# Softmax, normalising and gelu: small columns in one ring of buffers for each kind of column, where there was one ring for each width

## The chip, the cores and the metric

The kernel runs on one core of a Trainium2 chip. The metric is the device time in microseconds. It is one program, launched once. TensorE (PE) multiplies matrices into PSUM; VectorE (DVE), ScalarE (ACT) and GpSimd (POOL) do the rest, each from a queue of its own; SyncE (SP) issues transfers, and POOL issues the ones that gather or scatter rows.

## The reference

A gated block with cross-attention and a quantised feed-forward part, for 16 batches of 224 tokens with 512 numbers each, and a context of 750 rows of 384 numbers, of which a mask drops some:

```python
def _layernorm(x, axis=-1, eps=1e-05):
    m = jnp.mean(x, axis=axis, keepdims=True)
    v = jnp.var(x, axis=axis, keepdims=True)
    return (x - m) / jnp.sqrt(v + eps)

# _L0_xattn_ref: 8 heads of 64
q = (x @ W_q); k = (context @ W_k); v = (context @ W_v)
sim = jnp.where(mask, q k^T * scale, -max); attn = softmax(sim)
out = (attn @ v) @ W_o + b_o

# _L0_ffn_ref: both layers are bitlinear, with exact gelu between
def bitlinear(x, w, b):
    xq = act_quant(rmsnorm(x))     # scale 127 / max|x| of the row, rounded
    wq = weight_quant(w)           # -1, 0, 1 by the mean of |w|
    return jnp.einsum('bsd,fd->bsf', xq, wq) + b

x = x + jnp.tanh(g_xattn[0]) * _L0_xattn_ref(_layernorm(x), ctx_768, mask, ...)
x = x + jnp.tanh(g_ffn[0]) * _L0_ffn_ref(_layernorm(x), w1, b1, w2, b2)
return x
```

(The attention lines are shortened here.) What matters for the change is how many numbers there are of which each row has just one: a mean, a variance, a reciprocal of a softmax sum, a largest absolute value, a scale. Each is a column of 128 rows and one to six numbers.

## The kernel before

Batches are sorted by how many context rows their mask keeps. The eight fullest work with 192 key positions, the others with 128 (`CAPS`). If no batch has more, `compact_path` runs; it is the path that was profiled. It is one long list of instructions without loops on the chip.

The work is a pipeline of 16 stages, one for each batch `s`. A stage merges three streams of pieces by the costs written beside each piece (`merge`):

- `attention_pieces(s)`: softmax of the last two units of the batch and its weighted sum. A batch has four units `(s, n)`; a unit is 112 queries by four heads. `scores` (L1037) multiplies queries by keys, adds the mask with a running minimum on DVE (L1061), takes the exponential on ACT with its sum (L1071, `sum`), the reciprocal on DVE (L1080, `rec`) and multiplies by it on POOL (L1081). `turn_probs` transposes the result on TensorE (L1101, L1108).
- the `other` stream, which prepares later batches: `norm` (L944) for x of batch s+2, `gather` and `select` for its context rows, keys, values and queries for batch s+1. x comes in pairs of two 128-token tiles, by a gathering transfer that POOL issues (`fetch`, L793), into three buffers. `norm` takes statistics on DVE (`bs_x`, L952, then `mv_x`, L953), the scale and the negated mean on POOL (`rs_x`, `ls_x`, L956 to L959), and normalises x in place on POOL (L961).
- the `flow` stream. In stage 0 it rounds and transposes the weights w1, in stage 1 w2 (`weight_pieces`); `scale_weights` (L1371) adds the partial sums of |w| (`wtot`, L1373), spreads the total by a matmul with ones (L1375) and makes the scale; `round_weights` (L1392) and `turn_weights` (L1401) follow in eight pieces. From stage 2 on, it carries one pair of token tiles a stage through the feed-forward part: `residual`, `project` (L1184, output projection of the attention), `normalise` (L1213: `bs_y`, `mv_y`, `fx`, `a1`, `k`, the transposing transfer L1237, `r`, `c`), `up` (L1250), `gelu` (L1272: L1279 gelu on ACT, L1282 largest value `a2`, quantising, the transposing transfer L1288, L1290 squares on ACT with their sum `ss`, then `r2` and `c2` on POOL), `down` (L1300) and the scatter of the rows to the output (L1310).

After the last stage, the two last pairs are finished alone: `project` and `normalise` of pair 13, `up` and `gelu` of pairs 12 and 13, then `down`.

The order of the work on each engine is not written out in the kernel. The compiler takes the instructions in the order of the code as their priority, and moves a later one ahead when its inputs are ready and its engine has nothing to do by the compiler's own reckoning. A tile takes a buffer of its tag (its ring) when its first instruction is placed, and this can be only when a tile before it in that buffer has been read for the last time. [...]

All small columns come from one helper, which makes a tag of the width:

```python
    def small(name, n=2):
        return pa.tile([P, n], F32, tag=f"s{n}", name=name, bufs=24 if n == 2 else 6)
```

So there are three rings. The ring of two columns has 24 buffers and holds `rs`, `ls`, `k`, `c`, `a1`, `a2`, `r1`, `r2`, `ss`, `wtot`, `wmean`. The ring of four columns has six buffers and holds `mv` of x and of y, `sum` and `rec`. The ring of six columns has six buffers and holds `bs` of x and of y. PSUM has two wide buffers for scores, weighted sums and `up`, and four others (`gen`) for all else.

Of the kernel before, what the change touches and what calls it, by code (L numbers as in the profile page):

```python
# [8 lines left out]
F32 = mybir.dt.float32  # L9
# [716 lines left out]
def compact_path(ctx, tc, sh, x, context, out, late_loads):  # L726

    nc = tc.nc
    P = 128
    B, S, D = x.shape  # L730
    _, J, C = context.shape
# [17 lines left out]
    pa = ctx.enter_context(tc.tile_pool(name="pa", bufs=1))  # L749
# [21 lines left out]
    def wide(shape, dtype, name):  # L771
        return ps_sim.tile(shape, dtype, tag="sim", name=name)
# [6 lines left out]
    def pow_half(dst):  # L779
        nc.gpsimd.tensor_tensor(dst, dst, sh.mhalf[:, : dst.shape[1]], ALU.pow)  # L780

    def small(name, n=2):
        return pa.tile([P, n], F32, tag=f"s{n}", name=name, bufs=24 if n == 2 else 6)


    def token(t):
# [157 lines left out]
    def norm(i, ks=(0, 1)):  # L944

        xp = normed[i]
        name = f"x{i}_{ks[0]}"
        part = slice(ks[0], ks[-1] + 1)
        mv = small(f"mv_{name}", 4).rearrange("p (k n) -> p k n", k=2)
        for k in ks:  # L950
            st = small(f"bs_{name}_{k}", 6)
            nc.vector.bn_stats(st, xp[:, k, :])  # L952
            nc.vector.bn_aggr(mv[:, k, :], st)  # L953
            load["v"] += 850
        rstd = small(f"rs_{name}")
        nc.gpsimd.tensor_scalar(rstd[:, part], mv[:, part, 1], 1.0, EPS, ALU.mult, ALU.add)  # L956
        pow_half(rstd[:, part])
        less = small(f"ls_{name}")
        nc.gpsimd.tensor_scalar(less[:, part], mv[:, part, 0], -1.0, 0.0, ALU.mult, ALU.add)  # L959
        for k in ks:  # L960
            nc.gpsimd.tensor_scalar(  # L961
                xp[:, k, :], xp[:, k, :], less[:, k : k + 1], rstd[:, k : k + 1], ALU.add, ALU.mult
            )

    def norm_first(k):

        xp = normed[0]
        st = small(f"bs_x0_{k}", 6)
        nc.vector.bn_stats(st, xp[:, k, :])
        mv = small(f"mv_x0_{k}", 4)  # L970
        nc.vector.bn_aggr(mv[:, :2], st)
        rstd = small(f"rs_x0_{k}")
        nc.vector.tensor_scalar(rstd[:, :1], mv[:, 1:2], EPS, None, ALU.add)
        power = nc.gpsimd.tensor_tensor(rstd[:, :1], rstd[:, :1], sh.mhalf[:, :1], ALU.pow)
        nc.vector.tensor_scalar(xp[:, k, :], xp[:, k, :], mv[:, 0:1], rstd[:, :1], ALU.subtract, ALU.mult)
        return power.ins
# [60 lines left out]
    def scores(s, n):  # L1037
        st = live[s]
        cap = CAPS[s]
        q, u = UNITS[n]  # L1040
        sim = wide([TQ, 2, 2, 256], F32, f"sim_{s}_{n}")

        begin = P if cap > P else 0
        for i in range(2):
            p = 2 * u + i
            for j in range(2):
                nc.tensor.matmul(  # L1047
                    sim[:, j, i, :cap],
                    lhsT=st["qT"][j * DH : (j + 1) * DH, p, q * TQ : (q + 1) * TQ],
                    rhs=st["kT"][j * DH : (j + 1) * DH, p, j * begin : j * begin + cap],  # L1050
                    start=True,
                    stop=True,
                )
        probs = pa.tile([TQ, 4, 192], F32, tag="p", name=f"p_{s}_{n}", bufs=3)
        total = small(f"sum_{s}_{n}", 4)
        for i in range(2):
            for j in range(2):
                h = 2 * i + j
                nmax = pa.tile([TQ, 1], F32, tag="nm", name=f"nm_{s}_{n}_{h}", bufs=12)

                nc.vector.tensor_tensor_reduce(  # L1061
                    out=probs[:, h, :cap],
                    in0=sim[:, j, i, :cap],
                    in1=st["mask"][:, j * begin : j * begin + cap],
                    scale=-(DH**-0.5),
                    scalar=FMAX,
                    op0=ALU.add,
                    op1=ALU.min,
                    accum_out=nmax,
                )  # L1070
                nc.scalar.activation(  # L1071
                    probs[:, h, :cap],
                    probs[:, h, :cap],
                    AF.Exp,
                    bias=nmax,
                    scale=-1.0,
                    accum_out=total[:TQ, h : h + 1],
                )
        rec = small(f"rec_{s}_{n}", 4)
        nc.vector.reciprocal(rec[:TQ], total[:TQ])  # L1080
        nc.gpsimd.tensor_tensor(  # L1081
            probs[:, :, :cap],
            probs[:, :, :cap],
            rec[:TQ].unsqueeze(2).to_broadcast([TQ, 4, cap]),
            ALU.mult,
        )
        load["v"] += 4 * (150 + 1.05 * cap + 83) + 150
        load["s"] += 4 * (250 + 0.96 * cap + 187)
        st["p", n] = probs
# [106 lines left out]


    def quantiser(amax, part, least, name):
        k = small(f"k_{name}")
        nc.vector.tensor_scalar(k[:, part], amax[:, part], least, 1.0 / 127.0, ALU.max, ALU.mult)  # L1200
        nc.vector.reciprocal(k[:, part], k[:, part])
        load["v"] += 300
        return k

    def unquantiser(amax, r, part, isw, name):

        c = small(f"c_{name}")
        nc.gpsimd.tensor_tensor(c[:, part], amax[:, part], r[:, part], ALU.mult)
        nc.gpsimd.tensor_scalar(c[:, part], c[:, part], 1e-5, None, ALU.max)
        nc.gpsimd.tensor_scalar(c[:, part], c[:, part], isw, None, ALU.mult)  # L1210
        return c

    def normalise(i, ks=(0, 1)):  # L1213
        f = pairs[i]
        y = f["y"]
        name = f"{i}_{ks[0]}"
        part = slice(ks[0], ks[-1] + 1)
        mv = small(f"mv_y{name}", 4).rearrange("p (k n) -> p k n", k=2)
        if ks[0] == 0:
            f["fx"] = late["rows"].tile([P, 2, D], F32, tag="hq", name=f"fx_{i}", bufs=3)  # L1220
            f["xq"] = pa.tile([P, 2, D], BF16, tag="xq", name=f"xq_{i}", bufs=3)
            f["xqT"] = pa.tile([P, 2 * ND, P], BF16, tag="xq", name=f"xqT_{i}", bufs=3)
        fx, xq, xqT = f["fx"], f["xq"], f["xqT"]
        for k in ks:
            st = small(f"bs_y{name}_{k}", 6)
            nc.vector.bn_stats(st, y[:, k, :])
            nc.vector.bn_aggr(mv[:, k, :], st)
            nc.vector.tensor_scalar(fx[:, k, :], y[:, k, :], mv[:, k, 0:1], None, ALU.subtract)  # L1228
        amax = small(f"a1_{name}")
        nc.vector.tensor_reduce(amax[:, part], fx[:, part, :], AX.X, ALU.max, apply_absolute_value=True)  # L1230

        scale = quantiser(amax, part, 1e-5 * EPS, f"1_{name}")

        for k in ks:
            nc.vector.tensor_scalar(xq.bitcast(I16)[:, k, :], fx[:, k, :], scale[:, k : k + 1], None, ALU.mult)
        nc.vector.tensor_copy(xq[:, part, :], xq.bitcast(I16)[:, part, :])
        nc.sync.dma_start_transpose(  # L1237
            out=xqT[:, ks[0] * ND : (ks[-1] + 1) * ND, :], in_=xq[:, part, :].rearrange("p n d -> p (n d)")
        )

        r = small(f"r1_{name}")
        nc.gpsimd.tensor_scalar(r[:, part], mv[:, part, 1], 1.0 + EPS, EPS * EPS, ALU.mult, ALU.add)
        pow_half(r[:, part])
        c = unquantiser(amax, r, part, sh.isw[0], f"1_{name}")
        for k in ks:
            f["c1", k] = c[:, k : k + 1]
            nc.gpsimd.tensor_tensor(y[:, k, :], y[:, k, :], sh.b2, ALU.add)  # L1247
        load["v"] += len(ks) * (850 + 340 + 667 + 450 + 220)
# [23 lines left out]
    def gelu(i, ks=(0, 1)):  # L1272
        f = pairs[i]
        name = f"{i}_{ks[0]}"
        part = slice(ks[0], ks[-1] + 1)
        ss = small(f"ss_{name}")
        amax = small(f"a2_{name}")
        for k in ks:
            nc.scalar.activation(f["h", k], f["h", k], AF.Gelu)  # L1279
        for k in ks:  # L1280
# [7 lines left out]
            nc.sync.dma_start_transpose(out=hqT, in_=hq)  # L1288
        for k in ks:
            nc.scalar.activation(f["h", k], f["h", k], AF.Square, accum_out=ss[:, k : k + 1])  # L1290
        r = small(f"r2_{name}")
        nc.gpsimd.tensor_scalar(r[:, part], ss[:, part], 1.0 / FF, EPS, ALU.mult, ALU.add)
        pow_half(r[:, part])
        c = unquantiser(amax, r, part, sh.isw[1], f"2_{name}")
# [74 lines left out]
    weight_scale = [None, None]  # L1369

    def scale_weights(wi):  # L1371
        tot = small(f"wtot_{wi}")
        nc.vector.tensor_reduce(tot[:, 0:1], weight_sums[wi], AX.X, ALU.add)  # L1373
        pt = gen([P, 1], F32, f"wtotp_{wi}")
        nc.tensor.matmul(pt, lhsT=sh.ones, rhs=tot[:, 0:1], start=True, stop=True)  # L1375
        mean = small(f"wmean_{wi}")
        nc.vector.tensor_scalar(mean[:, 0:1], pt, 1.0 / (FF * D), 1e-5, ALU.mult, ALU.max)
        sw = pa.tile([P, 1], F32, name=f"sw_{wi}")
        nc.vector.reciprocal(sw, mean[:, 0:1])
# [205 lines left out]
```

## Time and profile before

| | |
|---|---|
| three timed runs | 758.72, 762.57, 763.36 us, median 762.57 |
| the profiled execution | 755.32 us, its span 753.5 us |
| mean granted TensorE clock | 0.976 |
| busy, share of the span | PE 90%, DVE 67%, ACT 54%, POOL 53% |
| instructions | PE 3902, DVE 1300, ACT 960, POOL 543 |
| read and written in HBM | 32.26 MB and 7.34 MB, 53 GB/s over the span |

The page divides the span in 40 slices of 18.8 us and gives each engine's busy share in tenths, with the clock that TensorE was granted (PEclk). The windows give the same as microseconds. In the timeline a line is start, duration, engine, line of the kernel and operation, with the tiles written and read; a number in square brackets is the time that the engine stood idle just before, and what ended it. Names of tiles there have lost their numbers, so `mv_x` stands for every pair of x. One and the same line of a helper can carry many operations: L766 and L763 are copies out of PSUM on ACT and DVE, L780 is the power of minus one half on POOL.

### The profile page before, as it was taken

Reading aid. Unit: us, or ns where it says so; the run is one execution under the profiler, and the core shown is the slowest. Engines: PE = TensorE matmul, PEld = TensorE weight load, DVE = VectorE, ACT = ScalarE, POOL = GpSimd, SP = SyncE. Lnnn points to the kernel's source line nnn. Section 1 sums busy time; section 2 is a strip of 40 time slices with the busy share of each in tenths; the row PEclk is TensorE's granted clock in tenths of the full one; section 3 lists DMA queues with packets and bytes.
Section 4 is the critical chain, followed back from the end, with each engine's and each line's share of the span. In section 5 each row is a group of like instructions: output and inputs, shape, how many; then the busy total and the mean of one; then the engine's idle time right before and its main releaser. Section 6 shows DMA issues by size and latency. Waiting matters only on the chain.

```text
span 753.5 us, 11378 instructions
## 1 busy us (share of the span) xinstructions
PE 680.1 (90%) x3902; PEld 432.9 (57%) x3902; DVE 505.9 (67%) x1300; ACT 407.6 (54%) x960; POOL 397.0 (53%) x543
## 2 busy tenths in 40 slices
PE   4997799999999999997999999999999999988652
PEld 3875587666566566555655575666666666443221
DVE  5598765877484784665768676588594939586860
ACT  1556564384663855736657369266565656460530
POOL 6583567464564644647266564565654453536141
PEclk9998999999999999999999999999999999999887
DMA  6874031132223322222142323123122222213150
GB/s 193 314 267 156 11 90 45 15 73 56 69 47 70 82 56 57 67 57 81 28 99 67 71 67 68 32 77 80 58 57 70 56 70 57 71 28 77 35 113 31
DMA packets 87218, 58.77 MB, mean 78 GB/s; under 512 B 75488, under 2 KB 75632, under 8 KB 87024
## 3 DMA queue, kind: packets, MB, share of 16 engines
q1 hardware_dynamic: 79024, 32.00, 18.8%
q0 software_dynamic: 8128, 25.96, 11.1%
q8 instruction: 33, 0.54, 0.3%
q14 instruction: 33, 0.27, 0.1%
HBM read 32.26 MB, written 7.34 MB: 53 GB/s over the span
## 4 chain that ended last, share of the span: by engine, by line
PE 57%; DVE 12%; issue 10%; POOL 9%; DMA 5%; ACT 2%; POOLq 0%; ACTq 0%; DVEq 0%; SPq 0%
PE qp L1008 9%; PE op L1189 9%; PE fp L1304 8%; PE hp L1259 6%; PE kp L892 5%; PE sim L1047 4%; PE vp L907 4%; PE ptp L1101 3%; PE av L1126 3%; DVE a L1282 2%; POOL p L1081 2%; DVE h L1267 2%; DMA raw<-in_L_ffn_w_dram 2%; DMA hqT<-hq 2%; DVE hq L1285 1%
## 5 line engine op out<-in xcount | busy, mean ns | idle before, releaser
L1081 POOL TENSOR_TENSOR p<-p,rec 112x768 f32<-112x768 f32 (+1 forms) x64 | 84.2, 1318 | 74.8 <-DVE rec L1080 29.6
L1304 PE MATMUL fp<-w2T,hqT 128*128 128x512 fp8e4 x448 | 104.2, 387 | 13.8 <-DMA hqT<-hq 13.7
L1259 PE MATMUL hp<-w1T,xqT 128*128 128x512 fp8e4 x448 | 107.0, 383 | 8.8 <-DVE h L1267 6.2
L1071 ACT ACTIVATE p<-p,nm 112x192 f32<-112x192 f32 (+1 forms) x256 | 106.4, 419 | 11.5 <-DVE nm L1061 11.3
L1008 PE MATMUL qp<-xnT,wq_sb 128*128 128x224 f32 x512 | 104.9, 358 | 0.6 <-ACT xnT L766 0.6
L1189 PE MATMUL op<-wo_sb,xoT 128*128 128x512 f32 x224 | 103.7, 599 | 0.0
L1008 PEld LDWEIGHTS qp<-xnT,wq_sb 128*128 128x128 f32 x512 | 96.8, 193 | 6.4 <-issue 3.3
L1267 DVE SCALAR_TENSOR_TENSOR h<-hp,c,b_bc 128x1024 f32<-128x1024 f32 x56 | 71.6, 1280 | 39.9 <-PE hp L1259 37.4
L1061 DVE CUSTOM_DVE_ANT_0 p<-sim,mask 112x192 f32<-112x192 f32 (+1 forms) x256 | 67.7, 319 | 33.9 <-PE sim L1047 33.4
L1304 PEld LDWEIGHTS <-hqT 128*128 128x128 bf16 x448 | 43.3, 99 | 71.0 <-DMA hqT<-hq 16.9
L1282 DVE TENSOR_REDUCE a<-h 128x1 f32<-128x2048 f32 x28 | 63.9, 2282 | 22.4 <-ACT h L1279 22.3
L1259 PEld LDWEIGHTS <-xqT 128*128 128x128 bf16 x448 | 43.2, 98 | 57.7 <-issue 15.4
L1308 DVE SCALAR_TENSOR_TENSOR y<-fp,c,y 128x512 f32<-128x512 f32 x28 | 20.9, 746 | 76.3 <-PE fp L1304 73.0
L1310 POOL DMA_INDIRECT out_dram<-y,token x28 | 30.9, 1104 | 75.6 <-DVE y L1308 70.6
L1290 ACT ACTIVATE h<-h 128x2048 f32<-128x2048 f32 x28 | 53.4, 1907 | 22.1 <-DVE hq L1285 14.7
L1279 ACT ACTIVATE h<-h 128x2048 f32<-128x2048 f32 x28 | 53.5, 1909 | 19.6 <-DVE k L1200 10.6
L1189 PEld LDWEIGHTS op<-wo_sb,xoT 128*128 128x128 f32 x224 | 40.6, 190 | 38.9 <-issue 36.4
L892 PE MATMUL kp<-ctxT,wk_sb 128*128 128x192 f32 (+1 forms) x384 | 60.9, 306 | 0.0
L892 PEld LDWEIGHTS kp<-ctxT,wk_sb 128*128 128x128 f32 x384 | 55.2, 192 | 6.2 <-issue 4.3
L1247 POOL TENSOR_TENSOR y<-y,b_bc 128x512 f32<-128x512 f32 x28 | 36.6, 1311 | 37.9 <-DVE fx L1228 37.6
L766 ACT COPY pT<-ptp 128x448 f32<-128x448 f32 x63 | 32.7, 536 | 42.6 <-PE ptp L1101 41.3
L1101 PE MATMUL ptp<-ident,p 112*128 112x112 f32 x256 | 36.1, 268 | 17.6 <-POOL p L1081 17.5
(165 smaller groups left out, 1191.4 us busy)
## 6 DMA issues: line engine op xcount, KB each, us to landing
raw<-in_L_ffn_w_dram SPq DMA_DIRECT2D x16, 512.0 KB, 5.6
wq_sb<-in_L_xattn_W_q_dram SPq DMA_DIRECT2D x1, 1024.0 KB, 5.8
b_bc<-in_L_ffn_b_dram SPq DMA_DIRECT2D x1, 1024.0 KB, 7.8
wk_sb<-in_L_xattn_W_k_dram SPq DMA_DIRECT2D x1, 768.0 KB, 7.4
wv_sb<-in_L_xattn_W_v_dram SPq DMA_DIRECT2D x1, 768.0 KB, 8.8
wo_sb<-in_L_xattn_W_o_dram SPq DMA_DIRECT2D x1, 512.0 KB, 3.8
wo_sb<-in_L_xattn_W_o_dram SPq DMA_DIRECT2D x2, 256.0 KB, 5.6
x<-in_x_dram,token POOLq DMA_INDIRECT x28, 3.6
```

The costliest lines, as they stand in the source:

```text
L892: nc.tensor.matmul(pk[:, p - p0, :], lhsT=sh.wk[:, c, p * P : (p + 1) * P], rhs=st["ctxT"][:, c, :cap], start=(c == 0), stop=(c == NC - 1),)
L1008: nc.tensor.matmul(pq[:, i, :], lhsT=sh.wq[:, d, (p + i) * P : (p + i + 1) * P], rhs=st["xnT"][:, d, :], start=(d == 0), stop=(d == ND - 1),)
L1061: nc.vector.tensor_tensor_reduce(out=probs[:, h, :cap], in0=sim[:, j, i, :cap], in1=st["mask"][:, j * begin : j * begin + cap], scale=-(DH ...
L1071: nc.scalar.activation(probs[:, h, :cap], probs[:, h, :cap], AF.Exp, bias=nmax, scale=-1.0, accum_out=total[:TQ, h : h + 1],)
L1081: nc.gpsimd.tensor_tensor(probs[:, :, :cap], probs[:, :, :cap], rec[:TQ].unsqueeze(2).to_broadcast([TQ, 4, cap]), ALU.mult,)
L1101: nc.tensor.transpose(pt[:, h, :], probs[:, h, c : c + P], ident[:TQ, :TQ])
L1189: nc.tensor.matmul(po, lhsT=xoT[:, d, at : at + P], rhs=sh.wo[:, d, :], start=(d == 0), stop=(d == ND - 1))
L1259: nc.tensor.matmul(ph[:, n, :], lhsT=f["xqT"][:, k * ND + d, :], rhs=w1T[:, d, at : at + NB], start=(d == 0), stop=(d == ND - 1),)
L1267: nc.vector.scalar_tensor_tensor(h[:, cols], ph.rearrange("t i n -> t (i n)"), f["c1", k], sh.b1[:, cols], ALU.mult, ALU.add)
L1279: nc.scalar.activation(f["h", k], f["h", k], AF.Gelu)
L1282: nc.vector.tensor_reduce(amax[:, k : k + 1], h, AX.X, ALU.max, apply_absolute_value=True)
L1304: nc.tensor.matmul(po, lhsT=f["hqT", k][:, n, :], rhs=w2T[:, n, :], start=(n == 0), stop=(n == NF - 1))
```

## The change

The helper takes a kind and a name. The kind is the tag, so each kind has a ring of its own, and every ring has six buffers, whatever its width. The rest of the change gives a kind to each call: `mvx`, `bsx`, `rsx`, `lsx` for x; `sum` and `rec` for softmax; `mvy`, `bsy`, `a1`, `k1`, `r1`, `c1` for the normalising; `ss`, `a2`, `k2`, `r2`, `c2` for gelu; `wtot` and `wmean` for the weights. These are 19 rings and 114 buffers, where there were three rings and 36 buffers. No operation, engine, operand or transfer is another.

```diff
-    def small(name, n=2):
-        return pa.tile([P, n], F32, tag=f"s{n}", name=name, bufs=24 if n == 2 else 6)
+    def small(kind, name, n=2):
+        return pa.tile([P, n], F32, tag=kind, name=f"{kind}_{name}", bufs=6)
...
-        mv = small(f"mv_{name}", 4).rearrange("p (k n) -> p k n", k=2)
+        mv = small("mvx", name, 4).rearrange("p (k n) -> p k n", k=2)
         for k in ks:
-            st = small(f"bs_{name}_{k}", 6)
+            st = small("bsx", f"{name}_{k}", 6)
...
-        rstd = small(f"rs_{name}")
+        rstd = small("rsx", name)
...
-        less = small(f"ls_{name}")
+        less = small("lsx", name)
...
-        total = small(f"sum_{s}_{n}", 4)
+        total = small("sum", f"{s}_{n}", 4)
...
-        rec = small(f"rec_{s}_{n}", 4)
+        rec = small("rec", f"{s}_{n}", 4)
...
-        k = small(f"k_{name}")
+        k = small("k" + name[0], name[2:])
...
-        c = small(f"c_{name}")
+        c = small("c" + name[0], name[2:])
...
-        mv = small(f"mv_y{name}", 4).rearrange("p (k n) -> p k n", k=2)
+        mv = small("mvy", name, 4).rearrange("p (k n) -> p k n", k=2)
...
-            st = small(f"bs_y{name}_{k}", 6)
+            st = small("bsy", f"{name}_{k}", 6)
...
-        amax = small(f"a1_{name}")
+        amax = small("a1", name)
...
-        r = small(f"r1_{name}")
+        r = small("r1", name)
...
-        ss = small(f"ss_{name}")
-        amax = small(f"a2_{name}")
+        ss = small("ss", name)
+        amax = small("a2", name)
...
-        r = small(f"r2_{name}")
+        r = small("r2", name)
...
-        tot = small(f"wtot_{wi}")
+        tot = small("wtot", wi)
...
-        mean = small(f"wmean_{wi}")
+        mean = small("wmean", wi)
```

The three columns of `norm_first`, which normalises the first pair of x at the very start, take the same kinds as those of `norm`.

More of the change, by code (lines that the diff above doesn't have):

```diff
@@ L967, in norm_first @@
         xp = normed[0]
-        st = small(f"bs_x0_{k}", 6)
+        st = small("bsx", f"x0_{k}", 6)
         nc.vector.bn_stats(st, xp[:, k, :])
-        mv = small(f"mv_x0_{k}", 4)
+        mv = small("mvx", f"x0_{k}", 4)
         nc.vector.bn_aggr(mv[:, :2], st)
-        rstd = small(f"rs_x0_{k}")
+        rstd = small("rsx", f"x0_{k}")
         nc.vector.tensor_scalar(rstd[:, :1], mv[:, 1:2], EPS, None, ALU.add)
```

## The prediction

> **What bounds the kernel now.** I read the page's busy times first, then its slices, then the windows of the early slices, and only then the order of single instructions in the timeline. All of it is one profiled execution of 755.32 us (span 753.5 us, the rest lies around it). The three timed runs have a median of 762.57, so I work out a difference and apply it to both.
>
> ```profile
> PE 680.1 (90%) x3902; PEld 432.9 (57%) x3902; DVE 505.9 (67%) x1300; ACT 407.6 (54%) x960; POOL 397.0 (53%) x543
> PE   4997799999999999997999999999999999988652
> PEclk9998999999999999999999999999999999999887
> ```
>
> TensorE is the bound nearly everywhere: 9 or more in 31 of 40 slices. It falls short at the start, in slices 4 and 5, in slice 19 and in the last six. A change of little columns on DVE, ACT and POOL can gain only where TensorE waits for them, so those slices are all there is to win. In the windows (columns: stretch, sum of the stretch, PE, PEld, DVE, ACT, POOL busy with counts, granted clock, DMA) the early shortfall is 5.1 us and 4.7 us, and the clock is short there as well:
>
> ```profile
> 56.50:75.30 18.80, 13.72 (x78) 9.58 (x77) 15.74 (x31) 12.19 (x29) 6.82 (x6) 0.82 0.49 156
> 75.30:94.20 18.90, 14.20 (x129) 10.86 (x128) 14.24 (x49) 11.22 (x33) 9.93 (x10) 0.91 0.04 11
> 113.00:131.90 18.90, 18.80 (x137) 14.28 (x135) 10.74 (x47) 9.23 (x30) 14.80 (x16) 1.00 0.16 45
> ```
>
> The stretch from 75.3 to 94.2 is the one the change touches. The timeline shows why TensorE waits there. First what is ready (columns: start, duration, engine, line):
>
> ```profile
> 72.59 1.28 DVE L952 BATCH_NORM_STATS2 bs_x<-x 128x6 f32<-128x512 f32 x2
> 74.82 1.06 ACT L1367 ACTIVATE junk<-raw 128x1024 f32<-128x1024 f32 x1 [0.57 <-DMA raw<-in_L_ffn_w_dram]
> 74.84 1.28 DVE L952 BATCH_NORM_STATS2 bs_x<-x 128x6 f32<-128x512 f32 x2
> ```
>
> The statistics of x pair 3 are done at 73.9 and those of pair 4 at 76.1; the last partial sum of w2 is read out at 76.0. Then what uses them:
>
> ```profile
> 83.76 0.17 DVE L1080 RECIPROCAL rec<-sum 112x4 f32<-112x4 f32 x1
> 83.84 0.22 DVE L953 BATCH_NORM_AGGREGATE mv_x<-bs_x 128x2 f32<-128x6 f32 x2
> 84.51 0.15 DVE L1373 TENSOR_REDUCE wtot<-wsums 128x1 f32<-128x8 f32 x1
> 84.81 0.35 PE L1375 MATMUL wtotp<-wtot,ones 128*128 128x1 f32 x2 [1.12 <-DVE wtot L1373]
> 89.23 1.03 PE L1413 MATMUL wp<-ident,w 128*128 128x128 bf16 x8 [3.57 <-DVE w L1398]
> ```
>
> Nothing in the data joins a softmax reciprocal to the mean of x or to the sum of w2, and DVE stood idle for 2.99 us before 80.1. What joins them is the ring. sum, rec, mv_x and mv_y share six buffers of four columns, and the compiled order gives them out in the order of the code: rec of unit (1,1), then mv of x pair 3. Behind that mv come its rs and ls, and behind those, in the ring of 24, the wtot of w2. So wtot stands 8 us after its last input, and TensorE waits 1.12 and 3.57 us. x pair 4 shows the same rule without any doubt; its statistics are 45 us old when the mean follows a reciprocal by 0.1 us:
>
> ```profile
> 120.77 0.18 DVE L1080 RECIPROCAL rec<-sum 112x4 f32<-112x4 f32 x1 [0.37 <-ACT p L1071]
> 120.86 0.22 DVE L953 BATCH_NORM_AGGREGATE mv_x<-bs_x 128x2 f32<-128x6 f32 x2
> ```
>
> **What the Trainium skill says.** *Perfetto Trace Analysis*, "Optimization Strategy": the same gap again and again on the engine that should be full can mean that no buffer was free for the next tile. The trace agrees for order and not for space: the 0.1 us behind rec. *TensorE: Matmul & The Clock Gate*, "What's actually happening": after about 3.4 us of idleness the array runs at half its clock until it has been busy that long. The trace agrees: the mean clock is 0.82 behind the 5.08 us gap at 57.8 and 0.91 behind the 3.57 us gap. The same page, "Architectural detail", calls DVE's queue strictly first in, first out, so one instruction that waits holds all behind it; the slower rival rests on that. *SBUF — State Buffer*, "Who interferes with whom": a cast on DVE and GpSimd work exclude each other. At 211.4 the cast of hq took 3.27 us, against a mean of 0.80, while POOL normalised x.
>
> **The change part by part.** No arithmetic, transfer or matmul is added or removed. The buffers grow by some 2.5 KB a partition (19 kinds of six, 32 B apart, against 36 buffers), and nothing is displaced by that. What changes is who waits for whose buffer, and through that the order in which the engines' queues are filled.
>
> Step 1, the early stretch. With mvx, rsx, lsx and wtot each in a ring of its own, wtot can follow the sum at 76.0. It won't come quite so early: its matmul takes a PSUM buffer after those of the key positions of batch 4, whose twelve matmuls stand at 80.84 to 81.42, so I put the matmul at about 81.5 instead of 84.81, 3.3 us earlier. The chain from there to the first transposed piece of w2 took 89.23 − 84.81 = 4.4 us, with softmax and index work in between; it would end near 85.9. TensorE has its score matmuls to 83.7 and the 0.63 us of x transposes that now wait behind wtotp, so about 1.5 of the 4.7 us of gap stay and 3.2 us go. The gap is then too short to bring the half clock. In slice 75.3 to 94.2 the lost clock is 18.9 × 0.09 = 1.7 us. Sum: 4.9 us. Bounds: 0 if the order of the PSUM ring holds the matmul where it is, 4.69 + 1.7 = 6.4 us if all of it goes. After 94 TensorE is full up to slice 11, so what is gained there is kept.
>
> Step 2, mv_x, rs_x and ls_x of the later pairs. They follow rec of unit (s,1) now. The x that they normalise is transposed a stage later, and the waits never name that as a late input of any length (ACT xnT 8.8 us in 11 is behind TensorE). Earlier is worth nothing: 0. The two DVE instructions (0.15 us each) and five on POOL (0.19 + 0.19 + 0.75 + 2 × 0.76 = 2.65 us) are the same work elsewhere.
>
> Step 3, bs_x and bs_y. They share six buffers, and bs_x of pairs 5 to 10, 12 and 13 comes within 1 us behind a bs_y that the code asks for earlier, some 20 to 75 us after its load. With rings apart, 2 × 0.68 us of DVE can go to the first idle moment after the load. Gain: the bs_x of 0.67 us at 374.6 stands right ahead of hq, whose transposed copy TensorE awaits at 383.05 for 0.93 us; 0.7 us. Loss: see the slower rival. I take 0 and keep −1 to +17 for the range.
>
> Step 4, mv_y, a1, k, r and c of the normalising, and ss, a2, k2, r2, c2 of gelu. mv_y follows rec of (s,3), which holds it by about 0.1 us for most pairs and by 12 and 8 us for pairs 0 and 7; a1 follows the last c of gelu in the order, but fx before it waits for an hq buffer in any case, and that ring is untouched. What they feed, up of the next stage, never waits for xqT in the list of waits. In the tail, mv_y of pair 12 stands at 676.0 with its statistics done at 674.9; the projection matmuls of pair 13 cover that until 692. 0, at most −1.
>
> Step 5, the tail from 692 on is a chain of amax, quantising, transposing DMA and down-projection with two h buffers. The small rings don't bind there. 0.
>
> Sum: −4.9 us, say −5: 750.3 for the profiled execution, 757.5 for the median.
>
> **The rivals.** *Slower: x statistics that stall DVE.* In the middle, POOL runs late against DVE at the start of each stage. In stage 4 the second multiply by rec runs at 205.43 though rec was done at 200.8, and the load of x pair 7 stands between the multiplies:
>
> ```profile
> 203.06 1.03 POOL L793 DMA_INDIRECT x<-in_x_dram,token  x1
> 205.43 1.48 POOL L1081 TENSOR_TENSOR p<-p,rec 112x768 f32<-112x768 f32 x1
> 205.69 2.29 DVE L1282 TENSOR_REDUCE a<-h 128x1 f32<-128x2048 f32 x1 [3.05 <-ACT h L1279]
> ```
>
> DVE idles 3.05 us before 205.69 for gelu, which is just where a free bs_x would be put. The load lands 3.6 us after its issue (median of the page), so at 206.7, and its second half at 208.0. Then amax starts at 207.4 at the least and at 208.7 at the most, 1.7 to 3.0 us late, and behind it wait the h of the other tile (TensorE's next PSUM buffer) and the scores of units (s,2) and (s,3). Seven pairs (7 to 13) at 2.5 us are 17 us; less the 5 of step 1, +12: 774.5. It decides once the stall that reaches TensorE is over 0.7 us a pair. For it: POOL lags by 3 to 5 us in stages 4 to 8, and DVE is in order. Against it: pairs 3 and 4 already have free statistics and wait for nothing; before 354.68 DVE idles 7.54 us anyway.
>
> *Faster by more.* The waits of transposes for POOL's multiply (17.5 us in all) and the other gaps over 0.3 us between 206 and 660 add up to 15.4 us, with 1.7 us of half clock behind the 3.47 us gap at 347. If the freer order takes x's 2.65 us on POOL away from the start of the stage, and from DVE's casts, half of that goes: −8.5 − 5 = −13.5: 749. Against it: x's work stands behind both multiplies now, not ahead.
>
> *Nothing kept.* The PSUM ring or DVE's softmax holds wtot back, or what step 1 wins is lost at the next wait: 762.5.
>
> **How the numbers follow.** Forecast 0.38 (757.5, own range 754 to 761), more 0.24, nothing 0.15, slower 0.23. A measurement of this kernel tells about 1% (7.6 us) from no change. Faster by over 1%: the faster rival and the lower edge of the forecast, 0.34. Slower by over 1%: most of the slower rival, 0.21. The rest, 0.45, within. The range goes from 744 to 776.
>
> **What would show it.** Right: wtot before 82.5, wp of w2 before 86.5, and no gap over 2 us or half clock between 80 and 94; mv_x directly behind bs_x everywhere. The slower rival: DVE waits for the load of x by L952, several times 1 to 4 us, and TensorE's gaps grow at the start of stages 4 to 12. Wrong: wtot still behind rec of (1,1), or a tail from 692 on that differs by over 3 us, which none of my steps allows.

## The result and the profile after

The changed kernel takes 782.14 us (median of four, 779.21 to 786.12), the kernel before beside it 760.64 (median of four). The ratio is 1.0322, with a 95% interval from 1.0278 to 1.0367: the change makes the kernel 3.2% slower, some 24 us; the two medians alone stand 21.5 us, 2.8%, apart. Ratios, here and below, are of fast executions alone, so they need not equal the quotient of the medians beside them. The forecast was 757.5, and the range ended at 776. The two profiled executions lie at opposite edges, 786.12 us (span 784.3) against 755.32 (span 753.5), so the traces differ by 30.8 us, of which some 7 to 9 are the choice of execution.

The page of the changed kernel, the same three rows as before:

```profile
PE 693.6 (88%) x3902; PEld 441.5 (56%) x3902; DVE 511.9 (65%) x1300; ACT 406.9 (52%) x960; POOL 395.7 (50%) x543
PE   4998898999899999997997978998999999889543
PEclk9989999999999999999998999999999999999785
```

The counts are the same. TensorE's busy time grew by 13.5 us with the same matmuls, which is a lower clock; the rest of the 30.8 us is waiting. Of the slices (19.6 us each, counted from 1), 22 and 24 have fallen to 7, and 7, 11, 25 and 28 to 8; 19 was weak before. The clock of the tail has a 7 and a 5. The windows of the early stretch and of two of the new weak places (stretch, length, PE, PEld, DVE, ACT, POOL busy, clock, DMA):

```profile
58.80:78.40 19.60, 17.02 (x138) 12.20 (x136) 17.36 (x39) 16.61 (x40) 9.77 (x11) 1.00 0.44 148
78.40:98.00 19.60, 17.13 (x130) 15.23 (x129) 16.71 (x52) 12.82 (x41) 11.17 (x12) 0.91 0.15 43
411.80:431.40 19.60, 15.00 (x55) 7.39 (x53) 18.05 (x41) 10.65 (x23) 8.38 (x13) 0.83 0.24 42
451.00:470.60 19.60, 15.54 (x89) 11.68 (x88) 10.80 (x31) 9.86 (x24) 8.70 (x12) 0.91 0.14 41
```

The early stretch has hardly gained, and from 411.8 on TensorE lacks 4.6 and 4.1 us in stretches that were full before. The list of waits (who waited, for whom, total us, times, longest) names a releaser that the kernel before did not have in the middle at all:

```profile
DVE bsx_x L952 <- DMA x<-in_x_dram,token: 39.6, 15, 8.8
POOL p L1081 <- DVE rec L1080: 39.0, 16, 9.2
ACT h L1290 <- DVE hq L1285: 36.9, 14, 6.3
PEld sim L1047 <- DVE h L1267: 15.5, 7, 4.7
PE sim L1047 <- DVE h L1267: 10.8, 4, 3.9
```

VectorE stands 39.6 us in fifteen waits of the statistics for the load of x. Behind them, the scores' matmuls on TensorE wait for `h` of VectorE, which they do only once in the kernel before:

```profile
PE sim L1047 <- DVE h L1267: 0.3, 1, 0.3
```

The two waits of POOL and ACT have grown (before 29.6 and 14.7 us), but the one of POOL is no sign of the loss: it is 45.2 us in run h2 below, which loses nothing in the middle. The timeline at 453 shows one such place whole (start, duration, engine, line, and in brackets the idle time before it and what ended it):

```profile
453.00 0.16 DVE L1080 RECIPROCAL rec<-sum 112x4 f32<-112x4 f32 x1
454.68 1.01 POOL L793 DMA_INDIRECT x<-in_x_dram,token  x1 [0.30 <-PE qp L1008]
456.92 1.03 POOL L793 DMA_INDIRECT x<-in_x_dram,token  x1 [0.16 <-issue]
458.07 0.69 DVE L952 BATCH_NORM_STATS2 bsx_x<-x 128x6 f32<-128x512 f32 x1 [4.90 <-DMA x<-in_x_dram,token]
460.26 0.69 DVE L952 BATCH_NORM_STATS2 bsx_x<-x 128x6 f32<-128x512 f32 x1 [1.28 <-DMA x<-in_x_dram,token]
461.08 1.25 DVE L1267 SCALAR_TENSOR_TENSOR h<-hp,c,b_bc 128x1024 f32<-128x1024 f32 x1
462.39 0.88 PE L1047 MATMUL sim<-kT,qT 64*112 64x128 f32 x8 [3.93 <-DVE h L1267]
```

The statistics stand in VectorE's queue right behind the reciprocal of 453.0, before POOL has even issued the load: the issues are at 454.68 and 456.92. VectorE waits 4.90 and 1.28 us, and all that time the `h` of 461.08, whose matmuls ended at 456.7, is queued behind it. That `h` frees the PSUM buffer of the next scores, so TensorE waits 3.93 us. The half clock follows; windows of just these gaps and of what comes after them:

```profile
414.90:418.80 3.90, 0.05 (x1) 0.00 (x0) 3.87 (x9) 1.12 (x1) 2.29 (x4) 0.95 0.00 0
418.80:422.80 4.00, 3.96 (x12) 2.17 (x13) 3.91 (x18) 3.97 (x5) 3.04 (x7) 0.50 0.66 89
458.50:462.40 3.90, 0.01 (x2) 0.01 (x2) 2.55 (x6) 0.82 (x2) 1.05 (x3) 1.00 0.23 67
462.40:466.40 4.00, 4.00 (x17) 2.08 (x18) 1.99 (x17) 3.97 (x7) 1.53 (x3) 0.57 0.02 4
```

Each gap of 3.9 us is followed by 4 us at about half clock, which costs another 2.0 us (4.0 × 0.50) and 1.7 us (4.0 × 0.43).

To see where the time goes over the whole run I take the start of the reciprocal of unit (s,n) on VectorE in two traces, and subtract the one before. The last column is the difference of the spans:

| kernel, less before, us | (2,3) | (7,1) | (8,1) | (8,2) | (9,2) | (12,0) | (15,1) | span |
|---|---|---|---|---|---|---|---|---|
| changed | 3.1 | 4.6 | 5.8 | 14.2 | 20.6 | 25.5 | 25.5 | 30.8 |

Three facts are in it. The early gain is not there at (2,3). Between there and (12,0), where the last pair of x is worked on, 22.4 us are lost, in steps that come right after the start of a stage. From (12,0) to (15,1) nothing is lost; the last statistics of x run at 525.2, ahead of (12,0). After that the tail loses about 5 us more.

The tail's part, in the timeline of the changed kernel:

```profile
726.75 4.48 DVE L1282 TENSOR_REDUCE a<-h 128x1 f32<-128x2048 f32 x2
731.53 2.48 DVE L1285 TENSOR_SCALAR hq<-h,k 128x2048 int16<-128x2048 f32 x2
732.91 1.91 ACT L1290 ACTIVATE h<-h 128x2048 f32<-128x2048 f32 x1 [4.11 <-DVE hq L1285]
736.46 1.44 PE L1259 MATMUL hp<-w1T,xqT 128*128 128x512 fp8e4 x3 [7.64 <-DVE h L1267]
```

and the same place in the kernel before:

```profile
701.34 2.29 DVE L1282 TENSOR_REDUCE a<-h 128x1 f32<-128x2048 f32 x1
704.04 1.28 DVE L1285 TENSOR_SCALAR hq<-h,k 128x2048 int16<-128x2048 f32 x1
705.42 1.91 ACT L1290 ACTIVATE h<-h 128x2048 f32<-128x2048 f32 x1 [2.03 <-DVE hq L1285]
708.72 2.27 DVE L1282 TENSOR_REDUCE a<-h 128x1 f32<-128x2048 f32 x1
708.85 1.01 PE L1259 MATMUL hp<-w1T,xqT 128*128 128x512 fp8e4 x2 [5.44 <-DVE h L1267]
```

Before, the largest value of pair 12's second tile came after the first tile had been quantised and squared. Now the two reductions run back to back (4.48 us for two), so hq of the first tile starts 4.8 us after the first reduction starts instead of 2.7. The squares that free the `h` buffer, the next `h` and TensorE's `up` all come some 2.1 us later.

### The profile page after: what moved, and what is told of

It is laid out like the page before. It is cut to its first block, busy times and chain, and to the rows that moved or that the text cites. A ratio compares the mean times of both kernels' runs of the same rounds, so it can differ in the third digit from the quotient of the medians.

```text
span 784.3 us, 11362 instructions
## 1 busy us (share of the span) xinstructions
PE 693.6 (88%) x3902; PEld 441.5 (56%) x3902; DVE 511.9 (65%) x1300; ACT 406.9 (52%) x960; POOL 395.7 (50%) x543
## 4 chain that ended last, share of the span: by engine, by line
PE 51%; DVE 15%; DMA 9%; issue 8%; POOL 7%; ACT 6%; POOLq 0%; ACTq 0%; SPq 0%; DVEq 0%
PE op L1189 9%; PE fp L1304 9%; PE qp L1008 7%; PE hp L1259 6%; PE kp L892 4%; PE vp L907 4%; DVE a L1282 4%; DMA x<-in_x_dram,token 3%; PE sim L1047 3%; DVE h L1267 3%; ACT p L1071 3%; PE av L1126 2%; POOL p L1081 2%; PE ptp L1101 2%; DMA raw<-in_L_ffn_w_dram 2%
## 5 line engine op out<-in xcount | busy, mean ns | idle before, releaser
L1259 PE MATMUL hp<-w1T,xqT 128*128 128x512 fp8e4 x448 | 108.8, 387 | 13.1 <-DVE h L1267 8.6
L1189 PE MATMUL op<-wo_sb,xoT 128*128 128x512 f32 x224 | 108.0, 620 | 0.0
L1259 PEld LDWEIGHTS <-xqT 128*128 128x128 bf16 x448 | 43.9, 99 | 63.4 <-issue 22.4
L892 PE MATMUL kp<-ctxT,wk_sb 128*128 128x192 f32 (+1 forms) x384 | 67.5, 326 | 0.1
L892 PEld LDWEIGHTS kp<-ctxT,wk_sb 128*128 128x128 f32 x384 | 61.2, 207 | 7.9 <-issue 4.9
L1047 PE MATMUL sim<-kT,qT 64*112 64x192 f32 (+1 forms) x512 | 51.3, 317 | 12.1 <-DVE h L1267 10.8
L1047 PEld LDWEIGHTS sim<-kT,qT 64*112 64x112 f32 x512 | 37.2, 174 | 32.4 <-DVE h L1267 15.5
```

What stands on the lines that cost most here:

```text
L892: nc.tensor.matmul(pk[:, p - p0, :], lhsT=sh.wk[:, c, p * P : (p + 1) * P], rhs=st["ctxT"][:, c, :cap], start=(c == 0), stop=(c == NC - 1),)
L1047: nc.tensor.matmul(sim[:, j, i, :cap], lhsT=st["qT"][j * DH : (j + 1) * DH, p, q * TQ : (q + 1) * TQ], rhs=st["kT"][j * DH : (j + 1) * DH, ...
L1189: nc.tensor.matmul(po, lhsT=xoT[:, d, at : at + P], rhs=sh.wo[:, d, :], start=(d == 0), stop=(d == ND - 1))
L1259: nc.tensor.matmul(ph[:, n, :], lhsT=f["xqT"][:, k * ND + d, :], rhs=w1T[:, d, at : at + NB], start=(d == 0), stop=(d == ND - 1),)
```

## The experiments

Theory A: what costs is the place of instructions in VectorE's queue. The rings had set it by accident: `bs` of x came late because its ring is given out in the order of the code, and the second tile's largest value came late for the same reason. Rivals: theory B, the freed order on GpSimd; and, for a rest of about 3 us, theory C (x's freed mean draws x's work on GpSimd ahead of other work there) and theory D (`r` and `c` of the normalising get another place on GpSimd). Times are beside the kernel before on the same chip, whose medians are 757.46 us for e1 to e4, 757.41 for f1, f2, f3 and h2, 756.9 for f6, h1 and h3, 757.25 for j1, and 759.24 for k1 and k2. Ratios have 95% intervals. e2 and e3 have four executions each, the others 12 to 22.

**One part put back (e1 to e4).** All edits are in the helper, with the 19 kinds as changed otherwise. From e3 on, the listings are shortened to the arguments that differ.

```diff
-        return pa.tile([P, n], F32, tag=kind, name=f"{kind}_{name}", bufs=6)
+        # e1: one ring of six for bs of x and of y
+        return pa.tile([P, n], F32, tag="bs" if n == 6 else kind, name=f"{kind}_{name}", bufs=6)
+        # e3: G = ("ss", "a2", "k2", "r2", "c2") in one ring of 24
+        tag="g" if kind in G else kind, bufs=24 if kind in G else 6
+        # e4: both
```

> The changed kernel, with bs of x and of y again in one ring of six; all other kinds stay apart. In the order of the queues this puts the x statistics of pairs 5 to 13 back to where they were before (behind the reciprocal of a unit (s,3), not behind that of (s,1) right after the load). Theory A (the x statistics stand in VectorE's queue ahead of the landing of their load): the 25 us that are lost by stage 12 go, the wait of L952 for the load (39.6 us in 15) falls below 3 us, and some 6 us of the tail stay: 753 to 762 us. Theory B (GpSimd's order: r and c of normalising among the columns of gelu, and mv_y, a1 placed earlier): that order is untouched here, so the loss stays: 775 to 785 us.

Measured: 764.68 us, ratio 1.0096 (1.0072 to 1.012). Against 1.0322 most of the loss is gone, and L952 no longer waits for a load. Theory B, which left the loss where it was, falls. The time is 2.7 us above the range I gave for A.

> The changed kernel, with ss, a2, k2, r2 and c2 of gelu together in one ring of 24; all else as changed. Theory A: it only puts the largest value of the second tile back behind the columns of the first, which takes away the tail's 7.64 us gap of TensorE at 728.8: 5 to 8 us less, 774 to 778 us, and the wait of L952 stays near 40 us. Theory B (columns of gelu are what costs): the middle comes back as well, 755 to 765 us.

Measured: 778.59 us, ratio 1.0318 (1.022 to 1.0416), just above the range given for A, with an interval too wide to tell it from the changed kernel. The trace is clearer: the tail's gap is 5.44 us again instead of 7.64, and L952 still waits 39.9 us.

> The changed kernel with both: bs of x and y in one ring, and gelu's five kinds in one ring of 24. What is left of the change is mv, sum, rec, rs, ls, a1, k1, r1, c1 and the weights' columns apart. Theory A: the two losses are separate places and add up, 782 - 24 - 6 = 752, with the early gain of w2 kept: 749 to 757 us, better than both kernels. If the early gain is lost again by stage 2 as in the changed kernel: 757 to 763 us. Theory B: over 770 us.

Measured: 761.09 us, ratio 1.0041 (1.0018 to 1.0064). The two cures add up, 0.55 points below e1, but not to a kernel better than before: the expected 749 to 757 is missed. The time lies in the 757 to 763 that I gave for an early gain that is lost again; what the early gain is worth is f1's question, and e4's own 0.41% is taken up further below.

**One part done alone, on the kernel before (e2, h1, f1, j1).** The rings that are set apart keep the number of buffers they had, 24 for two columns and six otherwise.

```diff
-        return pa.tile([P, n], F32, tag=f"s{n}", name=name, bufs=24 if n == 2 else 6)
+        # e2
+        tag="bsx" if name[:4] == "bs_x" else f"s{n}"
+        # h1
+        tag=name[:3] if name[:3] in ("ss_", "a2_", "k_2", "r2_", "c_2") else f"s{n}"
+        # f1
+        tag="w" if name[0] == "w" else f"s{n}"
+        # j1
+        tag="mv_y" if name[:4] == "mv_y" else name[:3] if name[:3] in ("a1_", "k_1", "r1_", "c_1") else f"s{n}"
```

> The kernel before, with one thing of the change alone: bs of x in a ring of its own. mv_x stays in the ring of four columns, so the mean, rs, ls and the normalising of x on GpSimd stay where they were before, and only the two statistics of each pair move ahead. Theory A: the wait of L952 for the load comes back with 30 to 45 us in about 15, and most of the 25 us with it, the tail is as before: 773 to 786 us. Theory B: GpSimd's order is as before, so 757 to 765 us. Between them, 765 to 773, would say that a part of the loss hangs on x's work on GpSimd moving along.

Measured: 773.68 us, ratio 1.0223 (1.0152 to 1.0295). This one ring, two statistics a pair and not a thing more, brings two thirds of the whole loss; e1, which puts the same ring back, takes 2.3 points off. Its waits, and the same place in its timeline as above:

```profile
DVE bs_x L952 <- DMA x<-in_x_dram,token: 39.2, 15, 7.6
PE sim L1047 <- DVE h L1267: 10.3, 3, 4.3
```

```profile
447.35 1.01 POOL L793 DMA_INDIRECT x<-in_x_dram,token  x1 [0.31 <-issue]
450.12 1.03 POOL L793 DMA_INDIRECT x<-in_x_dram,token  x1
450.57 0.69 DVE L952 BATCH_NORM_STATS2 bs_x<-x 128x6 f32<-128x512 f32 x1 [4.44 <-DMA x<-in_x_dram,token]
453.49 0.69 DVE L952 BATCH_NORM_STATS2 bs_x<-x 128x6 f32<-128x512 f32 x1 [2.22 <-DMA x<-in_x_dram,token]
454.10 1.27 DVE L1267 SCALAR_TENSOR_TENSOR h<-hp,c,b_bc 128x1024 f32<-128x1024 f32 x1
455.42 1.20 PE L1047 MATMUL sim<-kT,qT 64*112 64x128 f32 x8 [4.30 <-DVE h L1267]
```

The wait for the load is the same 39 us in 15, the chain load, statistics, `h`, scores is the same, and here x's mean, scale and normalising on GpSimd are where they were before. So it is the statistics on VectorE, not x's other work. By the second table below, 19.3 us of the trace are lost between (2,3) and (12,0), and nothing in the tail.

> The kernel before, with gelu's five kinds (ss, a2, k2, r2, c2) in rings of their own and nothing else of the change. The queues differ from the kernel before only from the last stages on: in the tail the largest value of pair 12's second tile stands directly behind that of the first, ahead of the first one's k and hq, where before it came behind c2 of the first. Theory A: hq of the first tile, its transposing transfer and the squares that free its h buffer come one reduction (2.2 us) later, and everything after is behind them: TensorE's gap of 5.44 us in the tail becomes 7.6 us, and two quantisings in a row push the later ones on: +4 to +7 us, 761 to 765 us where the kernel before takes 757.4. Rival, which is step 5 of the prediction (small rings don't bind in the tail): within 1 us, 756.5 to 758.5.

Measured: 760.28 us, ratio 1.0052 (1.0023 to 1.008), just under the range given for A, and outside the rival's in ratio (0.52% of 757 is 3.9 us). Its tail in the timeline:

```profile
699.94 4.48 DVE L1282 TENSOR_REDUCE a<-h 128x1 f32<-128x2048 f32 x2
704.72 2.48 DVE L1285 TENSOR_SCALAR hq<-h,k 128x2048 int16<-128x2048 f32 x2
709.66 1.44 PE L1259 MATMUL hp<-w1T,xqT 128*128 128x512 fp8e4 x3 [7.64 <-DVE h L1267]
```

The 7.64 us gap of the changed kernel comes with gelu's columns alone.

> The kernel before, with wtot and wmean alone in a ring of their own; GpSimd's order is untouched, TensorE's order changes only around the sum of w2. It is step 1 of the prediction by itself. Prediction: 5 us less, 752 to 753 us where the kernel before takes 757.5. Theory A: the traces of the changed kernel and of the run with bs and gelu in one ring each show the first piece of w2 2.3 us earlier, and then a new wait of 1.86 us for GpSimd's multiply of unit (1,3), because the four roundings of w2 now stand ahead of the softmax of units (1,2) and (1,3) on VectorE: the gain is given back by 102, so -1 to +1 us, 756.5 to 758.5.

Measured: 758.16 us, ratio 1.0015 (0.9992 to 1.0038): step 1 by itself is worth nothing that can be measured. In its trace the sum's matmul is at 80.66 and the first piece of w2 at 85.56, as step 1 said, with a gap of 2.53 us; then a gap of 1.26 us stands at 100.3, ahead of the transposes of unit (1,3).

> The kernel before, with the normalising's kinds alone (mv_y, a1, k1, r1, c1) in rings of their own: step 4 of the prediction by itself. TensorE's order is as before. It is the part of the change that no run has tried alone, and about 3 us of the change's loss are not yet placed. Step 4: 0 to -1 us, 756 to 757.5 where the kernel before takes 757. If it holds the missing 3 us (r of the normalising stands ahead on GpSimd and waits for mv_y, and the scatter and gathers wait behind it): 759 to 761 us.

Measured: 756.26 us, ratio 0.999 (0.997 to 1.0011): nothing, as step 4 said of these columns.

**The rings as changed, the place held (h2, h3).** All 19 kinds stay apart; the statistics of x, and their means with them, are queued behind the last reciprocal ahead of them in the code, that of unit (s,1).

```diff
-        nc.vector.reciprocal(rec[:TQ], total[:TQ])
+        load["rec"] = nc.vector.reciprocal(rec[:TQ], total[:TQ]).ins
...
-        name = f"x{i}_{ks[0]}"
+        name = f"x{i}_{ks[0]}"; hold = ExitStack(); hold.enter_context(tc.issue_after(load["rec"]))
...
-        rstd = small("rsx", name)
+        rstd = small("rsx", name); hold.close()
```

> The changed kernel with all 19 rings as they are; the only edit is that the statistics and means of x are queued on VectorE behind the reciprocal of unit (s,1) of the stage in which the code asks for them. Theory A (it is the place in VectorE's queue that costs, and the rings matter only because they set it): the wait of L952 for the load goes from 39.6 us to under 2, and the 22 us of the middle with it, and x's work on GpSimd is back after the reciprocal as well; the 4 to 7 us of the tail stay: 760 to 765 us. Rival (what costs is that the kinds of normalising, gelu and softmax no longer hold each other, wherever x's statistics are): 775 us or more.

Measured: 760.84 us, ratio 1.0022 (0.9988 to 1.0057). L952 waits for no load, and 22.4 us lost between (2,3) and (12,0) have become a gain of 1.4. The pair whose statistics waited at 453 in the changed kernel is loaded here at 437.89 and 440.13, and its statistics run 59 us later, without a wait:

```profile
499.38 0.16 DVE L1080 RECIPROCAL rec<-sum 112x4 f32<-112x4 f32 x1
499.46 1.25 DVE L952 BATCH_NORM_STATS2 bsx_x<-x 128x6 f32<-128x512 f32 x2
```

This is the sharpest of the runs: with not one ring put back the loss of the middle is gone. In the middle the rings as such cost nothing; the place does. The edit moves x's means, and so x's work on GpSimd, along with the statistics; that it is the statistics is what e2 adds.

> The changed kernel with both cures: statistics of x held behind the reciprocal of (s,1), and gelu's five kinds in one ring of 24. Theory A: the run with the hold alone (760.8) less the tail's 4 to 6 us: 754.5 to 757 us, level with the best so far or a little better than the kernel before. Rival (the tail's loss hangs on other kinds too): 759 to 761 us.

Measured: 756.72 us, ratio 0.997 (0.9937 to 1.0003): both losses cured, level with the kernel before or a little better.

**Where the last 3 us are (f2, f3, f6, k1, k2).** e4 was still 0.41% above the kernel before. From the kernel before, f3 sets `mv_x` apart; f6 sets `mv_x`, `rs_x`, `ls_x` and the weights' columns apart; k1 sets `sum` and `rec` apart; k2 joins f6's and j1's kinds, each in a ring of six. f2 is e4 with the ring of four as before.

```diff
+        # f3
+        tag="mvx" if name[:4] == "mv_x" else f"s{n}"
+        # f6
+        tag=name[:4] if name[:4] in ("mv_x", "rs_x", "ls_x") else "w" if name[0] == "w" else f"s{n}"
+        # k1
+        tag=name[:3] if name[:3] in ("sum", "rec") else f"s{n}"
```

> The changed kernel with the rings of four and of six columns as before (mv, sum and rec share six buffers, bs of x and y share six) and gelu's five kinds in one ring of 24. What is left of the change is rs, ls, a1, k1, r1, c1 and the weights' columns apart. The run with only bs and gelu put back was 3.1 us above the kernel before; it lost 8 us between the reciprocals of (8,1) and (10,2). Theory C (the mean of x, free of the reciprocals, draws x's 3 us on GpSimd ahead of the scatter and the gathers, so the multiplies of stages 9 and 10 come later): that goes, 755 to 758 us. Theory D (r and c of the normalising in another place on GpSimd): it stays, 760 to 762 us.

Measured: 756.37 us, ratio 0.9996 (0.9972 to 1.002). This is C's range; D, which left the loss where it was with `r1` and `c1` still apart, falls.

> The kernel before, with the mean and variance of x alone in a ring of their own; its statistics stay in the ring of six and so late. In the queues the mean follows its statistics, and x's scale and normalising on GpSimd come up to half a stage earlier. Theory C: 3 to 7 us lost in stages 8 to 10, 760 to 764 us. Theory D: GpSimd has time for it, 756 to 759 us.

Measured: 755.16 us, ratio 0.9974 (0.9954 to 0.9994). Theory C said 3 to 7 us slower; it is 2 us faster, the only run whose interval excludes 1 on that side. C falls as I put it.

> The kernel before, with mv, rs and ls of x and the weights' columns in rings of their own; statistics of x stay in the ring of six. It tells what lost 8 us between (8,1) and (10,2) in the run with only bs and gelu put back, and was not in the run with mv of x alone apart (755.2). Theory C' (x's normalising on GpSimd loses its place only when rs and ls are free too, and then stands ahead of the scatter and the gathers): 759 to 763 us. Theory D (it is mv_y, r1 and c1 of the normalising): 754 to 757 us.

Measured: 754.62 us, ratio 0.9993 (0.9967 to 1.0018). C' falls too, though the trace shows a part of it: 4.7 us go between (9,1) and (9,3), just after 2.6 us were gained, with a 2.45 us gap at 430.4 where the kernel before has 0.36.

> The kernel before, with sum and rec of the softmax in rings of their own; mv of x and of y share what is left of the ring of four, and are so freed from the reciprocals too. GpSimd's other columns stay in the ring of 24. If the missing 3 to 5 us lie in the softmax's columns: 760 to 762 us where the kernel before takes 757. If they lie in x's and the normalising's columns of two meeting on GpSimd: as the run with mv of x alone apart, 754 to 757 us.

Measured: 757.38 us beside 759.24, ratio 0.9995 (0.9967 to 1.0023).

> The kernel before, with mv, rs and ls of x, mv_y, a1, k1, r1 and c1 of the normalising and the weights' columns in rings of their own; sum and rec share six buffers, bs of x and y share six, gelu stays in the ring of 24. Against the run with only bs and gelu put back, only sum and rec share a ring again. If the two groups of columns, each harmless alone, cost when both are free on GpSimd: 759 to 762 us. If the softmax's columns were it: 754 to 757 us.

Measured: 757.91 us beside 759.24, ratio 0.9981 (0.9955 to 1.0007). Neither of the two holds it. No single group and no pair of groups that was tried costs what e4 costs above f2. This rest of 0.4% stays open; e4's interval begins at 0.18%, so it may be small. The trace of e4 shows where TensorE waits: 7.9 us go between (8,1) and (9,2), with gaps of 2.1 and 2.3 us at 394.6 and 434.3 before transposes of the softmax. At the second, x's scale and normalising run on GpSimd from 427.06 to 429.84, ahead of a scatter and two loads, and the multiply that TensorE needs comes 3.6 us after its reciprocal; in the kernel before, x's work stands behind both multiplies, and this one comes 1.2 us after its reciprocal. That is C's picture, but f6 has it too and is no slower in sum.

The table of above, for the runs on which the argument rests:

| kernel, less before, us | (2,3) | (7,1) | (8,1) | (8,2) | (9,2) | (12,0) | (15,1) | span |
|---|---|---|---|---|---|---|---|---|
| e1, bs in one ring | 3.7 | 1.2 | 1.5 | 3.6 | 6.9 | 7.3 | 7.4 | 12.5 |
| e4, bs and gelu put back | -1.9 | -4.1 | -5.4 | -1.0 | 2.5 | 3.7 | 3.7 | 4.2 |
| e2, only bs apart | -1.3 | 1.9 | 1.4 | 7.0 | 14.4 | 18.0 | 17.9 | 17.7 |
| h1, only gelu apart | -1.3 | -1.3 | -1.0 | -1.1 | -1.2 | -1.3 | -1.1 | 4.1 |
| h2, statistics held | 2.0 | -2.5 | -3.5 | -1.2 | -1.9 | 0.6 | 0.5 | 5.4 |
| f3, only mv_x apart | -3.7 | -4.7 | -5.4 | -4.3 | -4.5 | -4.6 | -4.7 | -3.4 |

Up to (2,3) a difference of some 3 us says little: the weights land at a different moment in each execution, and TensorE's gap near 61 was 5.08 us before, 2.58 in the changed kernel, 4.28 in e1 and 1.73 in f3.

The books, in per cent of the time before: statistics of x 2.23 (e2) and gelu's columns 0.52 (h1), each shown alone, and all other kinds together 0.41 (e4). That is 3.16 of 3.22, a closer fit than the intervals warrant, for e2's alone is 0.7 either way. Tried alone, the other kinds show nothing: the weights 0.15, the normalising -0.10, softmax's -0.05, x's mean, scale and negated mean together with the weights -0.07, with intervals that hold 0.

No version is clearly better than the kernel before. f3, one more ring for `mv_x`, is the only one whose whole interval lies below 1: 0.26% faster by the ratio, 755.16 against 757.41 us in medians, and by the two ratios 3.4% below the changed kernel. But f6 and k2 set `mv_x` apart too, and their intervals hold 1; among fourteen runs one such interval can be chance.

## Why the prediction was wrong

**What held.** That the rings are given out in the order of the code, and that the change would be felt through the order of the queues and through nothing else: the busy times of ACT and POOL moved by 1.3 us at most in the traces, and the 6.0 us that VectorE's grew are no loss in themselves (j1, which loses nothing, has 512.2 us). Step 1's mechanism: wtot came at 75.70, before the 82.5 that I asked for, its matmul at 80.82 (I said 81.5), the first piece of w2 at 85.66 (I said 85.9). Step 4's nothing for the normalising's columns (j1), but not for gelu's, which are the subject of step 5. And the slower rival's picture, down to the sign that it named: L952 waits for the load of x, several times over 1 us. TensorE's gaps do not grow in every stage from 4 to 12, though; the large new ones are in stages 8, 9 and 11.

**Step 3 failed.** I took 0 for `bs_x` apart from `bs_y`, with −1 to +17 kept for the range, and gave the rival that is this step's loss a chance of 0.23. The runs showed 2.23%, 17 us, for it alone. My rival priced it at seven pairs of 2.5 us. That the sum came out right is luck, for the shape was another: in e2's trace not an even 2.5 us a pair but at most 1.5 us a stage in stages 4 to 7, over 6 us in each of stages 8 and 9 and 3.6 us in stage 11. Where the wait reaches a score matmul it opens a gap (3.9 us twice in the changed kernel), and the half clock behind it adds 1.7 to 2.0. Two arguments set the chance too low. "Pairs 3 and 4 already have free statistics and wait for nothing" compared them with loads that had landed long before: pair 4's was issued at 57.66 and 58.98 and its statistics ran at 74.84, while in e2 the statistics of a later pair began at 450.57, 0.45 us after the issue of their second half. "Before 354.68 DVE idles 7.54 us anyway" counted idle time of VectorE as cover; but that idle time comes before `h` or the largest value, and a waiting instruction put there holds exactly these. What decides is not whether the engine is idle but when the instruction's input lands against when the next one's does: the profile of before had POOL issue that load 3 to 5 us late, with 3.6 us to landing, and so had the answer.

**Step 5 failed.** "The small rings don't bind there. 0." They did, and step 4's nothing for gelu's columns fell with it. In the timeline of before, gelu of the second tile is done at 703.4 and VectorE stands idle for 1.46 us before 707.52, yet the second reduction starts only at 708.72, 0.3 us after GpSimd first writes `c2` of the first tile. It is the trait that I had read off `mv_x` at 120.86, and did not look for in the tail. The term is 3.9 us (h1), not 0. That it is `a2` among gelu's five kinds that counts is read from the order; no run sets it apart alone. (The page's row also shows five weak slices at the end, not the six that I counted.)

**Step 1's size failed.** 4.9 us were worked out and about 0 measured (f1). "After 94 TensorE is full up to slice 11, so what is gained there is kept" is the sentence that was wrong. The timeline of the changed kernel:

```profile
80.82 0.38 PE L1375 MATMUL wtotp<-wtot,ones 128*128 128x1 f32 x2
85.66 0.62 PE L1413 MATMUL wp<-ident,w 128*128 128x128 bf16 x8 [2.47 <-DVE w L1398]
96.53 1.96 DVE L1396 TENSOR_SCALAR raw<-raw,sw 128x1024 f32<-128x1024 f32 x1
97.37 0.21 ACT L1071 ACTIVATION_READ_ACCUMULATOR p<-p,nm 112x1 f32 x1
99.35 0.16 DVE L1080 RECIPROCAL rec<-sum 112x4 f32<-112x4 f32 x1
99.66 2.76 POOL L1081 TENSOR_TENSOR p<-p,rec 112x768 f32<-112x768 f32 x1 [1.71 <-DVE rec L1080]
102.47 0.60 PE L1101 MATMUL ptp<-ident,p 112*128 112x112 f32 x4 [1.85 <-POOL p L1081]
```

w2 is 3.6 us earlier (the reciprocal of unit (1,1) stands 1.2 us earlier in this execution as well), but the reciprocal of unit (1,3) only 0.5 us (99.35 against 99.89). VectorE does both: it is busy without a break from 82.0 to 90.0 (3.70 of 3.70 us in the window to 85.7, 4.30 of 4.30 in the next), and roundings of w2 stand ahead of the softmax in its queue. The last sum of unit (1,3) is there at 97.6; its reciprocal comes 1.8 us later, behind the rounding that began at 96.53. So, as I read it, TensorE was full there before because VectorE was just ahead of it. Moved forward it catches up with VectorE and waits 1.85 us, after 2.47 us that stayed of the first gap. I had read "TensorE is full" as "TensorE is the bound". Nor did the half clock go, as I had said of a gap of 1.5 us: after the one of 2.47 us the clock was 0.70 over the next 4 us.

Last, my forecast added up what each step can give to TensorE, and kept the one step with a large loss in the range. For a change whose only effect is that a compiler is freer to move things, a loss that I could price and not exclude belonged in the forecast.

## What to carry to other kernels

A ring of buffers shared by tiles that have nothing in common is also an order: it tells the compiler what may not run ahead. Before you split one, list the instructions that it holds back, and ask of each what it will wait for if it is queued at the earliest place that a compiler finds free. One that waits for a late transfer, put ahead of the engine's next useful work, costs what of its wait reaches the busiest engine: in e2 39 us of waiting cost 17. If you want the rings apart, pin such instructions behind something whose time you know.

When a gain is worked out on the busiest engine, look at the engine that feeds it in the same stretch. If that one has hardly any idle time either, the gain ends where the two meet next.

## What the hardware showed that I had not expected

The half clock sets in after shorter gaps than the prediction took from the Trainium skill, *TensorE: Matmul & The Clock Gate*, "What's actually happening", which names about 3.4 us of idleness. In e4 the gap from 394.6 to 396.7, 2.1 us, is followed by 4 us at 0.57 of the clock. Its windows:

```profile
394.60:396.70 2.10, 0.01 (x1) 0.02 (x1) 2.06 (x2) 1.07 (x2) 2.07 (x3) 1.00 0.18 44
396.70:400.70 4.00, 4.00 (x14) 3.68 (x15) 3.74 (x5) 0.53 (x1) 3.54 (x3) 0.57 0.33 96
434.30:436.70 2.40, 0.07 (x2) 0.04 (x2) 0.06 (x1) 0.45 (x2) 2.14 (x3) 1.00 0.44 140
436.70:440.70 4.00, 4.00 (x20) 3.75 (x21) 0.00 (x0) 0.88 (x2) 3.44 (x3) 0.67 0.12 47
```

After the gap of 1.85 us at 100.6 in the changed kernel the clock stayed at 1.00, and after the one of 2.58 us at 61.4 as well, so there is no single threshold in these traces. A gap of 2.1 us cost 3.8 here: its own time and 4.0 × 0.43 of clock.
